# A selective-scan layer on one core: the chunks' preparation moved a batch ahead through DRAM, and one route less for the output sum

## The chip, the cores and the metric

The kernel runs on one core of one Trainium2 chip. The metric is the device time of one execution in microseconds (us). Engines are named as in the profile: PE (TensorE matmul), PEld (its weight loads), DVE (VectorE), ACT (ScalarE), POOL (GpSimd) and SP (SyncE, which issues every DMA of this kernel). Each engine works through its own queue strictly in the order in which the program was built; what one engine needs of another it waits for at that place of the queue.

## The reference

Two layers are computed for 8 images of 56 x 56 tokens and 192 channels. Layer 0 normalizes in groups, makes q with stride 1 and k, v with stride 2 (depthwise 3 x 3 convolution, affine, 1 x 1 convolution), attends with 3 heads, projects and adds. Layer 1 is a two-dimensional selective scan, cut here to what matters:

```python
xz = jnp.einsum('bhwc,oc->bhwo', x, in_proj_w)
xa, z = jnp.split(xz, 2, axis=-1)
xc = silu(depthwise_conv3x3(xa) + conv_b)              # 384 channels
# xs: four directions k: rows, columns, and both reversed
x_dbl = jnp.einsum('bkdl,kcd->bkcl', xs, x_proj_weight)
dts, Bs, Cs = jnp.split(x_dbl, [R, R + N], axis=2)     # R = 12, N = 16 states
delta = softplus(jnp.einsum('bkrl,kdr->bkdl', dts, dt_projs_weight) + dt_projs_bias)
def step(h, inp):
    u_l, d_l, B_l, C_l = inp
    h = exp(d_l[..., None] * A) * h + d_l[..., None] * B_l[:, :, None, :] * u_l[..., None]
    return (h, jnp.sum(h * C_l[:, :, None, :], axis=-1))
# y: the four directions' outputs brought back to one order, plus xs * Ds, and summed
y = layernorm(y) * out_norm_w + out_norm_b
x = x + einsum(y * silu(z), out_proj_w)
```

The scan has 3136 steps for each of 8 images, 4 directions, 384 channels and 16 states.

## The kernel before

**Tiling.** The 384 channels are three blocks of 128 partitions (NJ = 3). The 3136 tokens are seven chunks of 448 (NCH, T), a chunk is four pieces of 112 (SUB, TP). The main loop goes over 224 steps: batch, direction k, chunk. The reversed directions (k = 2, 3) go through the chunks backwards and through the columns of a chunk by negative strides. A state n of a chunk is a [128, 3 x 448] tile.

**One state.** SP loads row B_n, broadcast to 128 partitions (bb, L643, 4 buffers). POOL multiplies it with du = delta * u into dbu (L652, 3 buffers). ACT computes exp(A_n * delta) for each channel block into PSUM (da, L657, 2 banks). DVE runs the recurrence (tensor_tensor_scan, L659) from da and dbu into h (4 buffers); its last column is copied by ACT into newc (L662), the start of the next chunk. Then `add_state` forms sum over n of h * C_n in PSUM (y, one set of three banks), by one of three routes:

- BY_DVE, states 0, 6, 11: PE broadcasts row C_n to PSUM with a selection matrix (cm, L647), DVE multiplies h by it in place (L598), PE adds h to y through the identity (L604).
- BY_POOL, states 3, 8, 13: C_n is loaded broadcast (cb, L650), POOL multiplies in place (L601, once for each block), PE adds as above (L604).
- the other ten: for each of four pieces of 112 tokens PE transposes the three blocks of h into one bank (ht, L611), ACT copies that bank to SBUF scaled by C_n, which is now a per-partition scalar (g, L613), and PE transposes back and adds into y (L615).

After the last state DVE adds y into yacc, which holds the sum of directions in SBUF (L690 for direction 0, three instructions; L693 otherwise, one).

**Preparation.** `prepare` makes delta, du, B and C of one chunk of one direction while the chunk before it is scanned; it is a generator of which a piece is issued after every second state. It loads xs, projects (px, L553), copies to SBUF (xd, L555), stores the 32 rows of B and C to DRAM, transposes C (pct, L563; ct, L565), makes delta's argument (pdt, L573), and computes softplus as max(x, 0) + log(1 + exp(-|x|)) with a correction: on ACT L575 (Abs), L576 (Relu), L578 (Exp), L579 (Identity), L581 (Ln), on DVE L580, L582, L583 over [128, 3 x 448], and on POOL du (L585).

**Other work.** `front(b + 1)`, everything that comes before the scan for the next image (normalization, convolutions, attention, input projection and convolution), is a generator too. Each `yield` gives a cost; after every state the main loop issues pieces of it until the costs issued reach `total * (slot - first_slot) / (NTOK - NST - first_slot)`. So it is spread evenly over a batch's slots (a slot is one state): from the eighth chunk on (first_slot = 7 x 16) in batches after the first, from the first chunk in batch 0, and up to the last chunk but one. During direction 0, `finish(b - 1)` (layer norm, gate, output projection of the image before) is woven in, two pieces a state. All of these take PSUM from one pool of three banks. The framework derives all waits from the tiles and orders each engine's queue.

Of the kernel before, what the change touches and what calls it, by code (L numbers as in the profile page):

```python
# [18 lines left out]
L = HW * HW  # L19
# [20 lines left out]
BY_DVE = (0, 6, 11)  # L40
BY_POOL = (3, 8, 13)
EPS = 1e-5
CAP = 60.0
NTOK = NDIR * NCH * NST


@with_exitstack
def kernel(
# [56 lines left out]

    sel = fill("sel", [NR, len(BY_DVE), 128], 1.0)
    for i, n in enumerate(BY_DVE):
        nc.gpsimd.affine_select(out=sel[:, i], in_=sel[:, i], compare_op=ALU.is_equal, fill=0.0,
                                base=-(R + NST + n), pattern=[[0, 128]], channel_multiplier=1)

# [6 lines left out]
    xpw = load("xpw", [128, NDIR, NJ, NR], xp_wT.rearrange("k (j p) r -> p k j r", p=128))  # L117
# [35 lines left out]
    dchunk = ctx.enter_context(tc.tile_pool(name="dchunk", bufs=2, space=DRAM))  # L153
# [18 lines left out]
    s1 = ctx.enter_context(tc.tile_pool(name="s1", bufs=1))  # L172
    s2 = ctx.enter_context(tc.tile_pool(name="s2", bufs=2))
# [58 lines left out]
    def front(b):  # L232
# [184 lines left out]
        with tc.tile_pool(name=f"fw_{b}", bufs=1) as fw, tc.tile_pool(name=f"fi_{b}", bufs=2) as fi:  # L417
# [11 lines left out]
            made[b] = dict(x1d=x1d, xcs=xcs, rstd=rstd1, nbias=nbias)  # L429

            for j in range(NJ):
# [27 lines left out]
                for c in range(NCH):  # L459
                    xw = fi.tile([128, RPC, HW], F32, name="xw")  # L460
                    nc.gpsimd.tensor_copy(xw, xv.rearrange("p (h w) -> p w h", w=HW)[:, c * RPC:(c + 1) * RPC])
                    nc.sync.dma_start(xcs[1][:, j, c * T:(c + 1) * T], xw.rearrange("p a b -> p (a b)"))
                    yield 0.05

# [75 lines left out]
    dtws = {}  # L540

    def prepare(b, k, c, i):

        xs = s2.tile([128, NJ, T], F32, name="xs")
        nc.sync.dma_start(xs, made[b]["xcs"][k % 2][:, :, c * T:(c + 1) * T])
        if i == 0:
            dtw = s2.tile([R, DIN], F32, name="dtw")
            nc.sync.dma_start(dtw, dt_wT[:, k, :])
            dtws[k] = dtw
        yield {}  # L550
        px = bank("px")
        for j in range(NJ):
            nc.tensor.matmul(px[:NR, :T], xpw[:, k, j], xs[:, j], start=(j == 0), stop=(j == NJ - 1))  # L553
        xd = s2.tile([NR, T], F32, name="xd")
        nc.scalar.copy(xd, px[:NR, :T])  # L555
        rows = dchunk.tile([2 * NST, T], F32, name="rows")
        nc.sync.dma_start(rows, xd[R:NR, :])
        st = {"xs": xs, "xd": xd, "rows": rows}
        yield st

        pct = bank("pct")
        for s in range(SUB):
            nc.tensor.transpose(pct[:TP, s * NR:(s + 1) * NR], xd[:, s * TP:(s + 1) * TP], ident[:NR, :NR])  # L563
        ct = s2.tile([TP, SUB, NST], F32, name="ct")
        nc.scalar.copy(ct, pct[:TP, :SUB * NR].rearrange("p (s r) -> p s r", r=NR)[:, :, R + NST:NR])  # L565
        st["ct"] = ct

        dl = s2.tile([128, NJ, T], F32, name="dl")
        e = s1.tile([128, NJ, T], F32, name="e")
        ln = s1.tile([128, NJ, T], F32, name="ln")  # L570
        for j in range(NJ):
            pdt = bank("pdt")
            nc.tensor.matmul(pdt[:, :T], dtws[k][:, j * 128:(j + 1) * 128], xd[0:R, :], start=True, stop=True)  # L573
            q = k * NJ + j
            nc.scalar.activation(e[:, j], pdt[:, :T], AF.Abs, bias=dtb[:, q])  # L575
            nc.scalar.activation(dl[:, j], pdt[:, :T], AF.Relu, bias=dtb[:, q])  # L576
            yield st
        nc.scalar.activation(e, e, AF.Exp, scale=-1.0)  # L578
        nc.scalar.activation(ln, e, AF.Identity, bias=one)  # L579
# [178 lines left out]
```

## Time and profile before

| | us |
|---|---|
| median of 3 runs (21,996.19 to 22,010.04) | 21,998.8 |
| the profiled execution | 21,992.22 |
| its span, first to last instruction | 21,990.5 |
| mean granted TensorE clock | 0.92 |

| group (line) | instructions' count in the profile | busy us |
|---|---|---|
| POOL dbu L652 | 3584 | 10,845.1 |
| DVE scan L659 (with and without a start value) | 10,752 | 11,586.5 |
| ACT exp L657 | 10,752 | 6,795.8 |
| ACT g L613 | 8960 | 4,786.1 |
| POOL h*C L601 | 2016 | 2,508.1 |
| DVE h*C L598 | 672 | 1,035.9 |
| DVE L580, L582, L583 | 224 each | 432.9, 404.3, 344.7 |
| ACT L575, L576, L578, L579, L581 | 672, 672, 224, 224, 224 | 422.8, 424.1, 296.2, 316.3, 296.8 |
| POOL du L585 | 224 | 679.8 |

A row of the profile gives line, engine, operation, output and inputs by the program's names, shapes and count; then busy time and the mean of one in ns; then the idle time of the engine just before such instructions and what ended most of it. A matmul of float32 stands as two records (L604: 8064 records for 4032 instructions); one that only transposes stands as one. The ends of matmuls are modelled and records on PE and ACT overlap, so a group's mean is longer than its busy time over its count. A wait view names who waited for whom, with total, number and longest.

### The profile page before, as it was taken

The numbers are of one execution on the slowest core, as the hardware profiler recorded it, in microseconds if no ns is written. First come the engines' busy times: TensorE is split into PE (matmuls) and PEld (weight loads), VectorE is DVE, ScalarE is ACT, GpSimd is POOL, SyncE is SP. The second block draws the span as 40 slices with busy tenths as digits, with TensorE's granted clock in tenths as the row PEclk, the third lists the DMA queues.
The fourth block names the chain that finished last, engine by engine and source line by source line (L and its number), as shares of the span: only waits on it lengthen the run. The fifth ranks groups of instructions, "written<-read, shape, count | busy, mean of one in ns | idle before, by whom it ended". The sixth has DMA issues, their size and how long they took to land. (4 is left out here: it accounts for less than half of the span.)

```text
span 21990.5 us, 246125 instructions
## 1 busy us (share of the span) xinstructions
PE 18854.4 (86%) x84640; PEld 11005.3 (50%) x84640; DVE 15390.6 (70%) x14585; ACT 14548.1 (66%) x28166; POOL 14468.7 (66%) x6131
## 2 busy tenths in 40 slices
PE   8889888899888998889888899888988889887776
PEld 4454555545455455554555545555455554554444
DVE  1477777766677666876677766777667776677775
ACT  2467667666675766757666676666767667677665
POOL 0467677666676667766677666776667666677775
PEclk9899999999999999999999999999999999998888
DMA  1222222222222222222223222222222222222221
GB/s 50 82 66 66 67 84 65 74 62 65 82 68 71 63 69 77 81 61 61 73 75 80 60 62 73 76 77 62 61 84 68 76 61 61 81 70 67 61 61 41
DMA packets 935285, 1508.59 MB, mean 69 GB/s; under 512 B 102480, under 2 KB 917904, under 8 KB 930960
## 3 DMA queue, kind: packets, MB, share of 16 engines
q1 hardware_dynamic: 934032, 1492.83, 24.3%
q8 instruction: 670, 10.98, 0.2%
q14 instruction: 583, 4.78, 0.1%
HBM read 1322.38 MB, written 170.08 MB: 68 GB/s over the span
## 5 line engine op out<-in xcount | busy, mean ns | idle before, releaser
L652 POOL TENSOR_TENSOR dbu<-du,bb 128x1344 f32<-128x1344 f32 x3584 | 10845.1, 3040 | 4585.7 <-DVE h L659 2376.8
L659 DVE TENSOR_TENSOR_SCAN h<-da,newc,dbu 128x448 f32<-128x448 f32 x9216 | 10006.9, 1134 | 4142.2 <-PE ht L611 1467.0
L657 ACT ACTIVATE da<-dl,acoef 128x448 f32<-128x448 f32 x10752 | 6795.8, 638 | 3454.9 <-DVE h L659 3423.1
L613 ACT ACTIVATE g<-ht,ct 112x384 f32<-112x384 f32 x8960 | 4786.1, 576 | 1364.1 <-PE ht L611 1331.2
L615 PE MATMUL y<-ident,g 112*128 112x112 f32 x26880 | 4360.3, 281 | 1316.2 <-ACT g L613 1276.1
L611 PE MATMUL ht<-ident,h 128*112 128x128 f32 x26880 | 4483.0, 288 | 671.5 <-DVE h L659 182.1
L615 PEld LDWEIGHTS y<-ident,g 112*128 112x128 f32 x26880 | 2994.2, 147 | 3629.3 <-ACT g L613 3017.1
L604 PE MATMUL y<-h,ident 128*128 128x448 f32 x8064 | 3805.4, 611 | 473.2 <-DVE h L598 207.5
L611 PEld LDWEIGHTS ht<-ident,h 128*112 128x112 f32 x26880 | 3213.5, 141 | 1978.7 <-issue 1012.7
L601 POOL TENSOR_TENSOR h<-h,cb 128x448 f32<-128x448 f32 x2016 | 2508.1, 1272 | 1374.7 <-ACT newc L662 1374.7
L604 PEld LDWEIGHTS y<-h,ident 128*128 128x128 f32 x8064 | 1588.3, 211 | 2092.7 <-issue 1472.4
L659 DVE TENSOR_TENSOR_SCAN h<-da,dbu 128x448 f32<-128x448 f32 x1536 | 1579.6, 1072 | 676.2 <-PE ht L611 209.2
L662 ACT COPY newc<-h 128x3 f32<-128x3 f32 x3584 | 702.9, 196 | 1267.6 <-DVE h L659 1260.8
L215 PE MATMUL pcv<-xa,dg 128*128 128x440 f32 (+2 forms) x3024 | 1303.0, 545 | 0.3 <-ACT g L613 0.3
L388 PE MATMUL ps<-qT,kT 64*112 64x448 f32 x2352 | 1160.3, 605 | 70.3 <-DMA qT<-qd 38.3
L598 DVE TENSOR_TENSOR h<-h,cm 128x1344 f32<-128x1344 f32 x672 | 1035.9, 1542 | 255.8 <-PE cm L647 244.2
L396 PE MATMUL po<-pT,vt 112*128 112x448 f32 x2352 | 1043.1, 550 | 0.0
L585 POOL TENSOR_TENSOR du<-dl,xs 128x1344 f32<-128x1344 f32 x224 | 679.8, 3035 | 540.6 <-DVE dl L583 526.2
L391 ACT ACTIVATE pT<-ps,nsh 112x448 f32<-112x448 f32 x1176 | 726.1, 630 | 290.9 <-PE ps L388 237.8
L215 PE MATMUL pq<-band,dgq 96*96 96x440 f32 (+3 forms) x2016 | 866.4, 546 | 0.0
L647 PE MATMUL cm<-xd,sel 44*128 44x448 f32 x1344 | 712.0, 611 | 6.5 <-ACT dl L576 6.5
L573 PE MATMUL pdt<-xd,dtw 12*128 12x448 f32 x1344 | 708.0, 607 | 0.0
(140 smaller groups left out, 12929.0 us busy)
## 6 DMA issues: line engine op xcount, KB each, us to landing
bb<-rows SPq DMA_DIRECT2D x3584, 224.0 KB
cb<-rows SPq DMA_DIRECT2D x672, 224.0 KB
xt<-x1d SPq DMA_DIRECT2D x224, 336.0 KB
xs<-xch SPq DMA_DIRECT2D x112, 672.0 KB
xs<-xcw SPq DMA_DIRECT2D x112, 672.0 KB
xch<-xv SPq DMA_DIRECT2D x24, 1568.0 KB
xcw<-xw SPq DMA_DIRECT2D x168, 224.0 KB
xin<-in_x_dram SPq DMA_DIRECT2D x56, 336.0 KB
```

What stands on the lines that cost most here:

```text
L215: nc.tensor.matmul(out[:, o0:o1, a:b], lhs, img(lo, hi)[:, :, a + dx - 1:b + dx - 1], start=(t == TAPS[0]), stop=(t == TAPS[-1]))
L388: nc.tensor.matmul(ps[:TP, :T], kh[rows, kb * TP:(kb + 1) * TP], qh[rows, :], start=True, stop=True)
L396: nc.tensor.matmul(po[:, :T], vt[:, kb, g:g + 2, :].rearrange("p g d -> p (g d)"), pts[kb], start=(kb == 0), stop=(kb == NKB - 1))
L598: nc.vector.tensor_tensor(h, h, cm[:, :T].unsqueeze(1).to_broadcast([128, NJ, T]), ALU.mult)
L601: nc.gpsimd.tensor_tensor(h[:, j], h[:, j], cm, ALU.mult)
L604: nc.tensor.matmul(y[:, j, :T], ident, h[:, j], start=(n == 0), stop=(n == NST - 1))
L611: nc.tensor.transpose(ht[:TP, j * 128:(j + 1) * 128], h[:, j, cols], ident)
L613: nc.scalar.activation(g, ht[:TP, :DIN], AF.Copy, scale=ct[:, s, n:n + 1])
L615: nc.tensor.matmul(y[:, j, cols], g[:, j * 128:(j + 1) * 128], ident[:TP, :TP], is_transpose=True, start=False, stop=(n == NST - 1 and s = ...
L652: nc.gpsimd.tensor_tensor(dbu, du, bb.unsqueeze(1).to_broadcast([128, NJ, T]), ALU.mult)
L657: nc.scalar.activation(da[:, :T], dl[:, j], AF.Exp, scale=acoef[:, k * NJ + j, n:n + 1])
L659: nc.vector.tensor_tensor_scan(h[:, j, rev], da[:, 0:T][:, rev], dbu[:, j, rev], 0.0 if ci == 0 else carry[:, j, n:n + 1], ALU.mult, ALU.add)
```

## The change

What it does:

- `prepare` becomes `prep(b, lay, c, pools)`: one chunk in one layout (rows or columns) for both directions of that layout (k = lay and lay + 2). One projection serves both: xpw holds the two directions' weights side by side in 2 x 64 columns, so direction i's results lie on partitions 64 i and up; dtw is kept in SBUF in the same manner. The maximum max(x, 0) is computed by DVE, and so is the copy of ct. delta (dl), du, the rows of B and C, and ct are written to DRAM.
- The preps of image b + 1 (14: two layouts, seven chunks) run in the filler behind `front(b + 1)`, in the same even spread by costs; it ends a chunk earlier (NTOK - 2 * NST, and what is left is issued after the last chunk but two). Before the loop, `front(0)` and the first three preps of image 0 are issued; its other eleven come first in batch 0's filler.
- The scan loads each chunk's dl, du and ct from DRAM (`load_chunk`, at state 4 of the chunk before; xs too for direction 0).
- POOL writes du * B_n straight into an h tile, the scan runs in place, and there are ten h tiles (s8) in place of four h and three dbu.
- BY_DVE is gone, with its selection matrix and cm; BY_POOL is now states 0, 5, 10. The other thirteen take the transposing route. For BY_POOL states POOL, not ACT, copies newc.

```diff
-BY_DVE = (0, 6, 11)
-BY_POOL = (3, 8, 13)
+BY_POOL = (0, 5, 10)
 EPS = 1e-5
 CAP = 60.0
 NTOK = NDIR * NCH * NST
+HBUFS = 10
+LEAD = 3
...
+    xpw = fill("xpw", [128, 2, NJ, 2, 64], 0.0)
+    for k in range(NDIR):
+        nc.sync.dma_start(xpw[:, k % 2, :, k // 2, :NR], xp_wT[k].rearrange("(j p) r -> p j r", p=128))
+    dtw = const.tile([128, 2, DIN], F32, name="dtw")
+    for k in range(NDIR):
+        nc.sync.dma_start(dtw[k // 2 * 64:k // 2 * 64 + R, k % 2], dt_wT[:, k, :])
...
+            made[b] = dict(
+                x1d=x1d, xcs=xcs, rstd=rstd1, nbias=nbias,
+                dl=[dbatch.tile([128, NJ, L], F32, name=f"dl{k}") for k in range(NDIR)],
+                du=[dbatch.tile([128, NJ, L], F32, name=f"du{k}") for k in range(NDIR)],
+                rows=[dbatch.tile([2 * NST, L], F32, name=f"rows{k}") for k in range(NDIR)],
+                ct=[dbatch.tile([TP, L // TP, NST], F32, name=f"ct{k}") for k in range(NDIR)])
...
+    def prep(b, lay, c, pools):
+        p1, p2 = pools
+        m = made[b]
+        cols = slice(c * T, (c + 1) * T)
+        xs = p2.tile([128, NJ, T], F32, name="xs")
+        nc.sync.dma_start(xs, m["xcs"][lay][:, :, cols])
+        px = bank("px")
+        for j in range(NJ):
+            nc.tensor.matmul(px[:, :T], xpw[:, lay, j].rearrange("p k r -> p (k r)"), xs[:, j],
+                             start=(j == 0), stop=(j == NJ - 1))
+            yield 0.75
+        xd = p2.tile([128, T], F32, name="xd")
+        nc.scalar.copy(xd, px[:, :T])
+        pct = bank("pct")
+        for s in range(SUB):
+            nc.tensor.transpose(pct[:TP, s * 128:(s + 1) * 128], xd[:, s * TP:(s + 1) * TP], ident)
+        ct = p2.tile([TP, 2, SUB, NST], F32, name="ct")
+        nc.vector.tensor_copy(ct, pct[:TP, :].rearrange("p (s k r) -> p k s r", k=2, r=64)[:, :, :, R + NST:NR])
+        for i in range(2):
+            k = lay + 2 * i
+            nc.sync.dma_start(m["rows"][k][:, cols], xd[i * 64 + R:i * 64 + NR, :])
+            nc.sync.dma_start(m["ct"][k][:, c * SUB:(c + 1) * SUB], ct[:, i])
+        yield 0.5
+        dls, es = [], []
+        for i in range(2):
+            dls.append(p2.tile([128, NJ, T], F32, name="dl"))
+            es.append(p2.tile([128, NJ, T], F32, name="e"))
+        for j in range(NJ):
+            pdt = [bank("pdt") for _ in range(2)]
+            for i in range(2):
+                nc.tensor.matmul(pdt[i][:, :T], dtw[i * 64:i * 64 + R, lay, j * 128:(j + 1) * 128],
+                                 xd[i * 64:i * 64 + R, :], start=True, stop=True)
+            for i in range(2):
+                q = (lay + 2 * i) * NJ + j
+                nc.scalar.activation(es[i][:, j], pdt[i][:, :T], AF.Abs, bias=dtb[:, q])
+                nc.vector.tensor_scalar(dls[i][:, j], pdt[i][:, :T], dtb[:, q], 0.0, ALU.add, ALU.max)
+            yield 1.0
+        for i in range(2):
+            k = lay + 2 * i
+            e, dl = es[i], dls[i]
+            nc.scalar.activation(e, e, AF.Exp, scale=-1.0)
+            du = p2.tile([128, NJ, T], F32, name="du")
+            nc.scalar.activation(du, e, AF.Identity, bias=one)
+            nc.vector.scalar_tensor_tensor(e, du, -1.0, e, ALU.add, ALU.subtract)
+            yield 0.1
+            nc.scalar.activation(du, du, AF.Ln)
+            nc.vector.tensor_tensor(dl, dl, e, ALU.subtract)
+            nc.vector.tensor_tensor(dl, dl, du, ALU.add)
+            nc.sync.dma_start(m["dl"][k][:, :, cols], dl)
+            yield 0.1
+            nc.gpsimd.tensor_tensor(du, dl, xs, ALU.mult)
+            nc.sync.dma_start(m["du"][k][:, :, cols], du)
...
+    def load_chunk(b, k, c, i):
+        m = made[b]
+        cols = slice(c * T, (c + 1) * T)
+        dl = s2.tile([128, NJ, T], F32, name="dl_s")
+        nc.sync.dma_start(dl, m["dl"][k][:, :, cols])
+        du = s2.tile([128, NJ, T], F32, name="du_s")
+        nc.sync.dma_start(du, m["du"][k][:, :, cols])
+        ct = s2.tile([TP, SUB, NST], F32, name="ct_s")
+        nc.sync.dma_start(ct, m["ct"][k][:, c * SUB:(c + 1) * SUB])
+        xs = None
+        if k == 0:
+            xs = s1.tile([128, NJ, T], F32, name="xs_s")
+            nc.sync.dma_start(xs, m["xcs"][0][:, :, cols])
+        return dl, du, ct, xs
...
     def add_state(n, h, cm, y, ct):
 
-        if n in BY_DVE:
-            nc.vector.tensor_tensor(h, h, cm[:, :T].unsqueeze(1).to_broadcast([128, NJ, T]), ALU.mult)
-        elif n in BY_POOL:
+        if n in BY_POOL:
             for j in range(NJ):
                 nc.gpsimd.tensor_tensor(h[:, j], h[:, j], cm, ALU.mult)
...
+    def preps(b, todo):
+        es, pools = prep_pools(b)
+        with es:
+            for lay, c in todo:
+                yield from prep(b, lay, c, pools)
+    chunks = [(lay, c) for lay in range(2) for c in range(NCH)]
+    main = sum(front(0))
+    each = sum(preps(0, chunks[:LEAD])) / LEAD
...
+            late = preps(0, chunks[LEAD:]) if b == 0 else iter(())
+            fill = itertools.chain(front(b + 1), preps(b + 1, chunks)) if b + 1 < nb else iter(())
+            if b == 0:
+                fill = itertools.chain(late, fill)
+            total = main + len(chunks) * each + (each * (len(chunks) - LEAD) if b == 0 else 0.0)
...
-                dbu = s3.tile([128, NJ, T], F32, name="dbu")
+                    nc.sync.dma_start(cm, rows[NST + n, cols].partition_broadcast(128))
+                h = s8.tile([128, NJ, T], F32, name="h")
                 nc.gpsimd.tensor_tensor(
-                    dbu, du, bb.unsqueeze(1).to_broadcast([128, NJ, T]), ALU.mult)
-                h = s4.tile([128, NJ, T], F32, name="h")
+                    h, du, bb.unsqueeze(1).to_broadcast([128, NJ, T]), ALU.mult)
                 for j in range(NJ):
                     da = pa.tile([128, 512], F32, name="da")
                     nc.scalar.activation(da[:, :T], dl[:, j], AF.Exp,
                                          scale=acoef[:, k * NJ + j, n:n + 1])
                     nc.vector.tensor_tensor_scan(
-                        h[:, j, rev], da[:, 0:T][:, rev], dbu[:, j, rev],
+                        h[:, j, rev], da[:, 0:T][:, rev], h[:, j, rev],
                         0.0 if ci == 0 else carry[:, j, n:n + 1], ALU.mult, ALU.add)
-                nc.scalar.copy(newc[:, :, n:n + 1], h[:, :, last])
+                (nc.gpsimd.tensor_copy if n in BY_POOL else nc.scalar.copy)(newc[:, :, n:n + 1], h[:, :, last])
...
+            if n == 4 and i + 1 < len(steps):
+                nxt = load_chunk(*steps[i + 1])
...
-                want = total * (slot - first_slot) / (NTOK - NST - first_slot)
+                want = total * (slot - first_slot) / (NTOK - 2 * NST - first_slot)
...
-        if k == NDIR - 1 and ci == NCH - 2:
+        if k == NDIR - 1 and ci == NCH - 3:
```

## The prediction

> **What bounds the kernel now.** I read the page's totals first, then the busy time of the engines in the stages of one batch, then the rows of the costliest groups, and last the waits of a stage without foreign work.
>
> ```profile
> span 21990.5 us, 246125 instructions
> PE 18854.4 (86%) x84640; PEld 11005.3 (50%) x84640; DVE 15390.6 (70%) x14585; ACT 14548.1 (66%) x28166; POOL 14468.7 (66%) x6131
> ```
>
> No engine is full over the whole run, so the average does not say what an edit is worth. The stages do. A batch is 28 chunks of 16 states; the closing yacc instructions (L690, L693) mark where each ends. The next view sums busy time over stretches between such ends; columns are the stretch, its length, then PE, PEld, DVE, ACT and POOL busy, clock, DMA share, GB/s. The first three are batch 4: seven chunks of direction 0 with the previous batch's finish, the chunk in which the next batch's front starts, and 19 chunks with front work. The last is 20 chunks of batch 7: scan and preparation alone.
>
> ```profile
> 11381.70:11976.00 594.30, 500.55 (x2486) 313.77 (x2486) 474.96 (x457) 445.15 (x854) 469.33 (x196) 0.95 0.27 71
> 11976.00:12110.40 134.40, 97.50 (x482) 65.14 (x482) 98.44 (x116) 66.94 (x131) 73.84 (x32) 0.84 0.35 94
> 12110.40:13979.90 1869.50, 1671.62 (x7329) 944.39 (x7329) 1286.54 (x1194) 1253.16 (x2428) 1207.17 (x511) 0.94 0.24 67
> ...
> 20038.10:21730.10 1692.00, 1266.13 (x5960) 752.10 (x5960) 1298.11 (x1102) 1153.90 (x2300) 1227.09 (x522) 0.84 0.22 61
> ```
>
> Per chunk: 84.9 us in the first stage (PE fullest, 71.5), 98.4 in the third (PE 88.0, gap 10.4), 84.6 in the last (DVE 64.9, POOL 61.4, PE 63.3, ACT 57.7, so a gap of 20). Front chunks are near a PE bound; the others are held by waits between engines. In the last stage these are (us in total, times, longest):
>
> ```profile
> POOL dbu L652 <- DVE h L659: 230.0, 97, 4.2
> PEld ht L611 <- issue: 219.7, 257, 4.6
> DVE h L659 <- ACT da L657: 218.6, 167, 5.8
> PEld y L604 <- POOL h L601: 184.3, 180, 2.7
> ```
>
> PE waits in its queue for GpSimd's h*C (L601, behind multiplies that wait for one of three dbu tiles); the transposes behind it are late, then ACT's scaled copies, then the exponentials behind those, and the scan waits for ACT: some 11 us a chunk.
>
> **Scan, part by part.** Prices are busy time over count from these rows (records overlap a little, so I apply them to differences of measured busy time only):
>
> ```profile
> L613 ACT ACTIVATE g<-ht,ct 112x384 f32<-112x384 f32 x8960 | 4786.1, 576 | 1364.1 <-PE ht L611 1331.2
> L615 PE MATMUL y<-ident,g 112*128 112x112 f32 x26880 | 4360.3, 281 | 1316.2 <-ACT g L613 1276.1
> L611 PE MATMUL ht<-ident,h 128*112 128x128 f32 x26880 | 4483.0, 288 | 671.5 <-DVE h L659 182.1
> ...
> L604 PE MATMUL y<-h,ident 128*128 128x448 f32 x8064 | 3805.4, 611 | 473.2 <-DVE h L598 207.5
> ...
> L598 DVE TENSOR_TENSOR h<-h,cm 128x1344 f32<-128x1344 f32 x672 | 1035.9, 1542 | 255.8 <-PE cm L647 244.2
> ```
>
> Three states a chunk move from VectorE to the transposing route. PE gains 36 transpose pairs at 0.329 us, 11.8, and loses 18 matmul passes at 0.472, 8.5, and the cm broadcast, 3.2: nothing on balance. ACT gains 12 copies at 0.534, 6.4, and gives three newc copies (0.196 each) to GpSimd. DVE loses 4.6. The preparation leaves the chunk: 6.2 on PE, 8.6 on ACT, 7.4 on DVE (in the last stage), 3.0 on GpSimd. A 3-element copy on GpSimd is in no row: 0.1 us by its 1-element memsets, 0.48 by its 448-element ones; nearer to the first, 0.3. The scan in place keeps its shape, 1.08 us: nothing, hidden or not; at worst it is slower by what is unpriced here. What is left of a bare chunk: POOL 59.3, PE 57.2, ACT 54.9, DVE 52.9. The floor is 59.3 and the ceiling today's 84.6. Ten h tiles replace four h and three dbu, so the multiplies ahead of h*C no longer wait for a scan just done, but GpSimd still does h*C in turn, and PE and ACT still stand behind it three times a chunk: I take a gap of 12.7, so **72**. Direction 0: PE 71.5 - 6.1 = 65.4, POOL 64.9; gap 13 as today (84.9 - 71.5): **78.5**.
>
> **Where the preparation goes.** A prep (one chunk, two directions) now counts 6.35 units in the filler; the front counts 572. Together 661 units are spread over 19 chunks (7 to 25), where 572 had 20. So the front gets 16.4 chunks and all 14 preps are squeezed into 2.6, about chunks 24 to 26; the built order of the changed program shows them just there. But the units are PE time. A prep costs DVE 2 x (1.93 + 1.80 + 1.54) for L580, L582, L583 (their means over the run), 6 x 0.67 for the maximum that leaves ACT (nearest row: L442, same shape from PSUM; the other end is ACT's own 0.63) and 0.2 for ct: 14.8; ACT 12.4; PE 9; GpSimd 6.1. Three such chunks hold 3 x 52.9 + 14 x 14.8 = 366 us of DVE work and 338 of ACT work, 122 a chunk, where a chunk takes 98 today. 366 is the floor. The ceiling is the stage whose DVE is fullest today, the 134.4 us chunk, at 1.37 us per busy us: 500. Direction 0 has 1.19, bare chunks 1.30; I take 1.25: **457**. What is late next: PE idles there for lack of work, its front work having been done earlier, at a higher density.
>
> **Front chunks.** PE 88.0 - 6.1, and the front 20/16.4 denser: its share is 25 (88.0 - 63.3) to 35 (the rows of its lines, 5683 us over 8 x 20 chunks), so +5.4 to +7.6; I take 88.4. The gap is between 3 (y has one set of banks, and the built order puts yacc behind the first scan of state 9 of the next chunk, so the next y waits for a multiply, 3.0, that scan, 1.1, and yacc, 2.3, some 3 us more than PE has to do meanwhile) and today's 10.4. Ten tiles let the scan lead by nine states, which feeds PE; each ACT copy still stands in line with exponentials. I take 7.6: **96**. The chunk where the front starts loses 9.9 us of DVE: 125.
>
> A later batch: 7 x 78.5 + 125 + 16 x 96 + 457 + 72 = 2740, against 2683 as the mean of batches 1 to 6: +57, six times +342. Batch 7: 549.5 + 21 x 72 = 2061.5, against 2377.9: -316.
>
> **Batch 0** does 25 preps. Before its first scan stand two of them and a trip through DRAM, where one direction took 22.3 us:
>
> ```profile
> 738.83 0.53 ACT L555 COPY xd<-px 44x448 f32<-44x448 f32 x1 [13.68 <-PE px L553]
> ...
> 749.39 1.55 DVE L580 SCALAR_TENSOR_TENSOR e<-ln,e 128x1344 f32<-128x1344 f32 x1
> ...
> 761.16 2.07 DVE L659 TENSOR_TENSOR_SCAN h<-da,dbu 128x448 f32<-128x448 f32 x2 [3.58 <-POOL dbu L652]
> ```
>
> +10 (two DMA trips of 5.0, as xs took from its issue at 729.10 to PE's start on it at 734.11) to +60 (both preps in series): 36, first scan at 797. Eleven preps in the first three chunks: 1.25 x (3 x 52.9 + 163) = 402. Twenty front chunks at 88 (PE 88.4 less 7, as the front spreads over 20.3 chunks there, and a gap of 7) and 27 more for the one where it starts (125 against 98): 1787. Fourteen preps in four chunks: 1.25 x 419 = 524. One bare chunk. 3582, against 3328.9: +253.
>
> **DMA, SP, constants.** Writing and reading dl and du adds 617 MB and the shared xs saves 39: q1 goes from 24.3% to about 34%, no bound. SP issues about 217 instead of 60 of these per batch, all in order: in a prep chunk its stores, waiting for DVE and GpSimd, stand between the bb loads. Four bb tiles cover 12 us; that is part of the 1.25. The constants' eight small loads for two lie under the first front's 740 us of other work: nothing, or some 5 us (one DMA trip) without that cover.
>
> [...] L580 takes 1.55 alone, 1.93 on average, and in bare chunks
>
> ```profile
> L580 DVE SCALAR_TENSOR_TENSOR e<-ln,e 128x1344 f32<-128x1344 f32 x20 | 87.7, 4385 | 3.9 <-ACT ln L579 3.9
> ```
>
> which is one GpSimd multiply (3.04) more. [...]
>
> **Sum.** +342 + 253 - 316 = +279 on the span of 21,990.5: 22,269.5, and 1.7 outside it as in the profiled run (21,992.2 in all), 22,271. The median, 21,998.8, is 6.6 above that run; I leave it out.
>
> **Rivals.** *Ten tiles close the gaps* (faster): one mechanism, the lead of the scan. Gap 4.6 in front chunks (93), 10 in direction 0 (75), 9 in bare ones (68), preps at 1.05: a batch 2583, batch 0 3368, batch 7 1953; 21,007. For it: waits, not work, fill the gaps. Against: GpSimd's h*C stays in all queues. It decides once front chunks (116 of them) average under 93.5, other terms as forecast. *The chain of a prep binds* (slower still): dl, e and du have two buffers, both used by one prep, so the next waits for its stores: 16.0 us from xd to dl (738.83 to 754.9), 3.0 du, 5.0 store, 6 for the second direction is 30 on idle engines, 40 in queues; 14 x 40 = 560 for 457, and 25 x 7.4 in batch 0: 23,073. Against: the region overlaps preps' ends. *The tiles stay unused*: GpSimd's newc copy and h*C wait for the scan in its own queue, chunks stay 84.6 and 84.9: +28 x 12.6 + 49 x 6.4, 22,938. Against: in bare chunks the built order puts ten multiplies ahead of the first copy.
>
> **How the numbers follow.** Forecast 0.37, long chain 0.13, unused tiles 0.09: slower 0.59. Closed gaps 0.33. Within 0.2% (44 us, about what this measurement can tell) 0.08: forecast and rival in balance. Range 21,300 to 23,000; the forecast's own, preps at 1.15 to 1.4 of 2937 us, is 21,980 to 22,710.
>
> **What would show it.** Chunks 24 to 26 of a middle batch at 140 to 165 us with DVE over 115 busy; front chunks at 94 to 98, bare ones 68 to 76, direction 0 76 to 81; batch 7 near 2060. Prep chunks under 130 us or front chunks under 93 make it wrong.

## The result: slower by 16%, and the profile after

The changed kernel takes 25,476 us (median of 4 runs, 25,455 to 25,496) against 22,000.5 for the kernel before (4 runs): a ratio of 1.158, 95% interval 1.156 to 1.160. The direction is the one that had most of the chance; the time lies far outside the range.

The page's totals of the changed kernel:

```profile
span 25453.5 us, 275939 instructions
...
PE 19586.6 (77%) x94272; PEld 12662.8 (50%) x94272; DVE 15296.1 (60%) x14697; ACT 15379.5 (60%) x29174; POOL 14650.3 (58%) x6800
```

DVE and POOL have about as much to do as before, ACT 6% more, and all three are less full: what grew there is waiting. The stages of batch 4, cut within 3 us of the ends of the yacc instructions (columns: stretch, length, then PE, PEld, DVE, ACT and POOL busy, clock, DMA share, GB/s): seven chunks of direction 0, the chunk where the next front starts, 15 front chunks, three chunks that hold the preps; the last line is 21 bare chunks of batch 7, with neither front work nor preps.

```profile
13708.80:14280.40 571.60, 454.63 (x2718) 337.85 (x2718) 416.10 (x413) 428.60 (x840) 446.25 (x210) 0.90 0.33 88
14280.40:14423.40 143.00, 99.11 (x540) 70.19 (x538) 102.01 (x129) 76.44 (x156) 69.46 (x39) 0.84 0.32 91
14423.40:16230.00 1806.60, 1439.66 (x6541) 902.28 (x6542) 888.02 (x885) 988.87 (x1933) 897.05 (x434) 0.87 0.22 63
16230.00:16770.00 540.00, 381.32 (x1338) 218.14 (x1337) 413.34 (x322) 333.81 (x521) 303.35 (x118) 0.65 0.39 130
23833.00:25266.00 1433.00, 1032.25 (x6933) 742.22 (x6933) 1118.34 (x1030) 1164.13 (x2372) 1207.38 (x579) 0.95 0.30 81
```

Per chunk, by the ends themselves, forecast in brackets: direction 0 81.8 (78.5); first front chunk 143 (125); front chunks 120.3 (96); the three prep chunks 540 (457); bare chunks 68.2 (72). Batches 1 to 6 take 3189 on average (2740), batch 0 4125 (3582), batch 7 2007 (2061.5). So the bare chunks went even better than foretold, and of the 452 us by which batch 4 was missed 328 stand in its front chunks and the bare ones at its end together (15 of 120.3 and two of 65.6, where 16 of 96 and one of 72 were foretold), 83 in the preps, 41 in the first eight chunks. A front chunk holds 96.0 us of PE and a gap of 24.3; 88.4 and 7.6 were foretold.

The two rows of product and scan show what is late:

```profile
L687 POOL TENSOR_TENSOR h<-du_s,bb 128x1344 f32<-128x1344 f32 x3584 | 11025.8, 3087 | 8189.4 <-PE ht L638 3294.4
L693 DVE TENSOR_TENSOR_SCAN h<-da,newc,h 128x448 f32<-128x448 f32 x9216 | 10063.5, 1135 | 7307.8 <-POOL h L687 5595.9
```

Product and scan last about as long as before (3.09 us for 3.04, 1.14 for 1.14); the idle time in front of them is new. GpSimd's product waits for PE, the scan for the product.

### The profile page after: what moved, and what is told of

The parts are those of the page before. It is cut to its first block, busy times and chain, and to the rows that moved or that the text cites. A ratio compares the mean times of both kernels' runs of the same rounds, so it can differ in the third digit from the quotient of the medians.

```text
span 25453.5 us, 275939 instructions
## 1 busy us (share of the span) xinstructions
PE 19586.6 (77%) x94272; PEld 12662.8 (50%) x94272; DVE 15296.1 (60%) x14697; ACT 15379.5 (60%) x29174; POOL 14650.3 (58%) x6800
## 5 line engine op out<-in xcount | busy, mean ns | idle before, releaser
L687 POOL TENSOR_TENSOR h<-du_s,bb 128x1344 f32<-128x1344 f32 x3584 | 11025.8, 3087 | 8189.4 <-PE ht L638 3294.4
L693 DVE TENSOR_TENSOR_SCAN h<-da,newc,h 128x448 f32<-128x448 f32 x9216 | 10063.5, 1135 | 7307.8 <-POOL h L687 5595.9
L691 ACT ACTIVATE da<-dl_s,acoef 128x448 f32<-128x448 f32 x10752 | 6796.2, 637 | 5512.6 <-DVE h L693 5474.5
L642 PE MATMUL y<-ident,g 112*128 112x112 f32 x34944 | 6119.0, 297 | 2989.5 <-ACT g L640 2927.0
L640 ACT ACTIVATE g<-ht,ct_s 112x384 f32<-112x384 f32 x11648 | 6192.4, 574 | 1686.8 <-PE ht L638 1499.7
L642 PEld LDWEIGHTS y<-ident,g 112*128 112x128 f32 x34944 | 4262.5, 158 | 5787.6 <-ACT g L640 4984.6
L638 PE MATMUL ht<-ident,h 128*112 128x128 f32 x34944 | 6287.1, 304 | 1021.0 <-ACT pT L393 217.6
L638 PEld LDWEIGHTS ht<-ident,h 128*112 128x112 f32 x34944 | 4535.6, 149 | 2273.4 <-issue 900.5
L631 PE MATMUL y<-h,ident 128*128 128x448 f32 x4032 | 2014.5, 634 | 541.3 <-DVE yacc L725 290.2
L693 DVE TENSOR_TENSOR_SCAN h<-da,h 128x448 f32<-128x448 f32 x1536 | 1573.6, 1072 | 1203.2 <-POOL h L687 915.9
```

What stands on the lines that cost most here:

```text
L631: nc.tensor.matmul(y[:, j, :T], ident, h[:, j], start=(n == 0), stop=(n == NST - 1))
L638: nc.tensor.transpose(ht[:TP, j * 128:(j + 1) * 128], h[:, j, cols], ident)
L640: nc.scalar.activation(g, ht[:TP, :DIN], AF.Copy, scale=ct[:, s, n:n + 1])
L642: nc.tensor.matmul(y[:, j, cols], g[:, j * 128:(j + 1) * 128], ident[:TP, :TP], is_transpose=True, start=False, stop=(n == NST - 1 and s = ...
L687: nc.gpsimd.tensor_tensor(h, du, bb.unsqueeze(1).to_broadcast([128, NJ, T]), ALU.mult)
L691: nc.scalar.activation(da[:, :T], dl[:, j], AF.Exp, scale=acoef[:, k * NJ + j, n:n + 1])
```

## Experiments

### Where the front chunks' time went: a closed ring

Each single run below had the kernel before beside it, at 21,980 to 22,057 us, so differences of some 0.3% between single runs tell nothing.

The waits in 15 front chunks, first of the kernel after, then in the 19 of the kernel before (who waited for whom; total us, times, longest):

```profile
DVE h L693 <- POOL h L687: 841.3, 212, 8.6
ACT da L691 <- DVE h L693: 576.0, 354, 6.3
PEld y L642 <- ACT g L640: 371.0, 392, 5.9
POOL h L687 <- PE ht L638: 315.8, 71, 11.4
```

```profile
ACT da L657 <- DVE h L659: 344.7, 394, 6.6
PEld y L615 <- ACT g L613: 270.4, 414, 4.3
POOL dbu L652 <- DVE h L659: 262.1, 108, 9.6
DVE h L659 <- PE ht L611: 235.0, 106, 8.9
```

Before, GpSimd's product waited mostly for the scan, and the scan for PE. Now the product waits for PE, and the scan for the product. The timeline of the kernel after in two such states (start, length, instruction, in brackets the idle time before it and who ended it):

```profile
15203.13 3.23 DVE L693 TENSOR_TENSOR_SCAN h<-da,newc,h 128x448 f32<-128x448 f32 x3 [4.51 <-POOL h L687]
...
15207.74 0.42 PE L638 MATMUL ht<-ident,h 128*112 128x128 f32 x1
...
15208.30 3.03 POOL L687 TENSOR_TENSOR h<-du_s,bb 128x1344 f32<-128x1344 f32 x1 [5.20 <-ACT da L691]
...
15211.36 3.23 DVE L693 TENSOR_TENSOR_SCAN h<-da,newc,h 128x448 f32<-128x448 f32 x3 [5.00 <-POOL h L687]
15212.55 0.64 ACT L691 ACTIVATE da<-dl_s,acoef 128x448 f32<-128x448 f32 x1 [1.39 <-DVE h L693]
...
15213.96 2.42 PE L631 MATMUL y<-h,ident 128*128 128x448 f32 x6
...
15216.46 3.04 POOL L687 TENSOR_TENSOR h<-du_s,bb 128x1344 f32<-128x1344 f32 x1 [5.14 <-PE y L631]
...
15219.53 3.23 DVE L693 TENSOR_TENSOR_SCAN h<-da,newc,h 128x448 f32<-128x448 f32 x3 [4.94 <-POOL h L687]
```

PE ends a state's last transpose at 15208.16; 0.14 us later the product starts (the view names an exponential of ACT there, which no product reads), and 0.03 us after the product's end at 15211.33 the scan. The next product starts 0.08 us after PE's six passes over an h tile. Product and scan take turns, 8.2 us a state, each engine idle for 5.

My theory: a tile that the product and the scan share is freed by PE's read. In front chunks PE runs behind, and the built order lets the scan's queue run nine states ahead of PE's, the whole ring of ten tiles (they are used in turn, so a state writes over the tile of the state ten earlier). Then product (s + 10) waits for PE's read of state s, scan (s + 10) for the product, the exponentials behind it for the scan, and ACT's scaled copies g, which stand in ACT's queue behind those exponentials, hold PE. (In the trace of the changed kernel the instructions that name a tile, 14,697 on DVE, 29,013 on ACT and 6796 on GpSimd, all stand in the built order.) In bare chunks PE follows one or two states behind, and the ring should hold nothing up.

The trace of the changed kernel shows the wait itself. By the order of their records, 85% of the products of these 15 chunks start within 0.5 us of PE's last read of the state ten earlier (median 0.14 us, none sooner than 0.08). In bare chunks 45% do so too, but there the scan leads PE by 2.0 states on average, for 9.6 in front chunks, and the products run some eight ahead of the scan, so it doesn't wait for them.

Four runs tell the theory from its rivals. The first takes back the sharing in the changed kernel:

```diff
-HBUFS = 10
+HBUFS = 7
-                h = s8.tile([128, NJ, T], F32, name="h")
+                dbu = s3.tile([128, NJ, T], F32, name="dbu")
                 nc.gpsimd.tensor_tensor(
-                    h, du, bb.unsqueeze(1).to_broadcast([128, NJ, T]), ALU.mult)
+                    dbu, du, bb.unsqueeze(1).to_broadcast([128, NJ, T]), ALU.mult)
+                h = s8.tile([128, NJ, T], F32, name="h")
...
-                        h[:, j, rev], da[:, 0:T][:, rev], h[:, j, rev],
+                        h[:, j, rev], da[:, 0:T][:, rev], dbu[:, j, rev],
```

> The changed kernel with the scan out of place again: GpSimd's product goes to one of three dbu tiles, the scan writes one of seven h tiles (ten tiles in all, as in the changed kernel). Theory (closed ring): in the changed kernel the product for state s+10 may not start before PE has read state s, so product (3.1 us), scan (1.1 to 3.4), exponential and scaled copies stand in series with PE, about 7.5 us a state. Out of place, the product waits only for the scan three states earlier: front chunks fall from 120 to 95..102 us, the whole from 25,476 to 23,000..23,700. Rival (three more states on the transposing route load ACT's queue and PE): front chunks stay at 115 or more, the whole within 1.5% of 25,476. Bare chunks tell how much of their 68 us is owed to the place: with the ring open there, 68..70 by the theory.

Measured, one run: 22,597 us. The stages of batch 4, 15 front chunks and three prep chunks, and 21 bare chunks of batch 7:

```profile
12646.70:14088.60 1441.90, 1274.33 (x6544) 797.17 (x6544) 887.24 (x884) 984.89 (x1932) 897.27 (x434) 0.96 0.28 79
14088.60:14578.50 489.90, 368.29 (x1340) 215.15 (x1340) 380.52 (x322) 334.10 (x522) 293.00 (x112) 0.68 0.44 142
20800.60:22409.00 1608.40, 1126.15 (x6930) 798.10 (x6930) 1116.96 (x1028) 1165.57 (x2370) 1222.02 (x585) 0.87 0.27 73
```

Two of its waits in front chunks (12,649 to 14,166 us):

```profile
DVE h L694 <- PE ht L638: 387.0, 153, 28.6
POOL dbu L687 <- DVE h L694: 301.2, 117, 18.4
```

The product waits for the scan again, and the scan for PE. Front chunks take 96.1 us, as the theory had it; the whole lies below its 23,000, since the preps (490 for 540), direction 0 (79.3) and batch 0 (3686) gained too. The bare chunks speak against it in one point: 76.6, not 68 to 70. That is taken up below. The second run shortens the lead without opening the ring:

```diff
-HBUFS = 10
+HBUFS = 5
```

> The changed kernel with five h tiles for ten. Theory (closed ring): the built order uses up whatever tiles there are (the scan's queue leads the transposes by four states instead of nine), so the product still stands behind PE's read of the state five earlier, and front chunks stay at 112..130 us, the whole at 25,000..26,500. Rival (a lead of nine states is too long, ACT's scaled copies stand behind too many exponentials): with a lead of four, front chunks come near the 98.4 of the kernel before, the whole to 23,000..23,700.

Measured, one run: 25,574 us. The same two stages, 15 front chunks and 21 bare ones:

```profile
14469.60:16285.30 1815.70, 1442.83 (x6540) 900.02 (x6540) 883.93 (x884) 986.34 (x1930) 897.48 (x434) 0.87 0.22 63
23945.70:25382.80 1437.10, 1037.73 (x6930) 744.05 (x6930) 1116.97 (x1027) 1163.13 (x2370) 1221.44 (x584) 0.95 0.31 82
```

121.0 and 68.4 us a chunk: half the tiles make no difference of note anywhere. Between five and ten, it is neither the length of the lead nor the number of tiles; with five, 86% of the products of front chunks start within 0.5 us of PE's read of the state five earlier. The next two change one part each in the kernel before: product and scan share its seven tiles; and no h*C on VectorE, with GpSimd's three states moved to 0, 5 and 10.

```diff
+    s8 = ctx.enter_context(tc.tile_pool(name="s8", bufs=7))
...
-                dbu = s3.tile([128, NJ, T], F32, name="dbu")
+                h = s8.tile([128, NJ, T], F32, name="h")
                 nc.gpsimd.tensor_tensor(
-                    dbu, du, bb.unsqueeze(1).to_broadcast([128, NJ, T]), ALU.mult)
-                h = s4.tile([128, NJ, T], F32, name="h")
+                    h, du, bb.unsqueeze(1).to_broadcast([128, NJ, T]), ALU.mult)
...
-                        h[:, j, rev], da[:, 0:T][:, rev], dbu[:, j, rev],
+                        h[:, j, rev], da[:, 0:T][:, rev], h[:, j, rev],
```

> The kernel before with another part of the change alone: the product and the scan share one of seven h tiles (as many as four h and three dbu). Theory (closed ring): front chunks rise from 98.4 to 112..122 us, the whole to 23,500..24,600, and the wait of the scan for GpSimd's product appears as the largest one. Rival (place does not matter; preparation or the transposing route does): within 2% of 22,000.

```diff
-BY_DVE = (0, 6, 11)
-BY_POOL = (3, 8, 13)
+BY_DVE = ()
+BY_POOL = (0, 5, 10)
```

> The kernel before with one part of the change alone: no h*C on VectorE (those three states go the transposing route), GpSimd's three states are 0, 5 and 10. Theory (closed ring by the scan in place): here the product still goes to dbu, freed by the scan, so front chunks stay at 95..103 us for 98.4 and the whole within 2% of 22,000 (21,700..22,400). Rival (the longer transposing route is what costs): front chunks at 115..120, the whole at 24,000..24,700.

Measured, one run each: 24,120 and 21,450 us, beside 21,986 for the kernel before. Sharing alone costs 2134 us. Its stretch of 15 front chunks, and two of its waits there:

```profile
13376.10:15114.00 1737.90, 1480.35 (x5834) 824.06 (x5834) 1010.38 (x964) 1010.63 (x1950) 921.37 (x393) 0.85 0.20 54
```

```profile
DVE h L659 <- POOL h L653: 640.6, 149, 10.1
...
POOL h L653 <- PE ht L612: 314.0, 79, 11.5
```

115.9 us a chunk, with the two waits of the changed kernel, though preparation, routes and number of tiles are those of the kernel before. The longer transposing route is no loss but a gain of 2.4%: 18 front chunks of batch 4 take 95.3 us for 98.6, bare ones 81.0 for 84.1, direction 0 88.7 for 84.9. Repeated, to have an interval:

> The kernel before without h*C on VectorE again, to have an interval: 21,450 +-0.3%, a ratio of 0.975 +-0.003 to the kernel before.

21,432 us (median of 4 runs), ratio 0.974, interval 0.973 to 0.976. Taken apart in this order, the parts come to about -0.54 thousand (the route), +1.15 (preparation ahead, its room and GpSimd's newc: 22,597 less 21,450) and +2.88 (sharing: 25,476 less 22,597; alone in the kernel before it was 2.13).

### Why bare chunks got 68 us: the order in GpSimd's queue

```diff
-HBUFS = 7
+HBUFS = 5
-                dbu = s3.tile([128, NJ, T], F32, name="dbu")
+                dbu = s3.tile([128, NJ, T], F32, name="dbu", bufs=5)
```

> The changed kernel out of place, with five dbu and five h tiles for three and seven. Theory (the lead of the products): bare chunks took 68 us in place and 77 out of place because GpSimd's products could run ten states ahead and here only three; with five, bare chunks fall to 69..73, batch 7 from 2169 to 2010..2090, while front chunks stay at 93..98 since the product still waits for a scan, not for PE; the whole 22,250..22,480. Rival (it is the scan's lead of nine states that fills the bare chunks): bare chunks stay at 76 or more, or rise, as the scan's lead falls to four.

Measured, one run: 22,578 us, bare chunks 76.2, front chunks 96.3. The products' lead is not it, against the theory, and neither is the scan's: with five tiles for ten the changed kernel had 68.4. The timeline of GpSimd with three dbu and seven h tiles, in a bare chunk:

```profile
21518.29 0.19 POOL L697 COPY newc<-h 128x3 f32<-128x3 f32 x1 [0.99 <-DVE h L694]
21518.44 3.03 POOL L687 TENSOR_TENSOR dbu<-du_s,bb 128x1344 f32<-128x1344 f32 x1
21521.42 3.32 POOL L629 TENSOR_TENSOR h<-h,cb 128x448 f32<-128x448 f32 x3
```

Between newc and h*C of one state the built order puts a product: the scan that ends frees a dbu tile too, and h*C, which overwrites h, also waits for the copy. So h*C comes 3.0 us late, three times a chunk. In the changed kernel a scan's end frees no tile for a product, and in its bare chunks h*C follows at once:

```profile
24518.62 0.19 POOL L696 COPY newc<-h 128x3 f32<-128x3 f32 x1 [0.67 <-DVE h L693]
24518.89 3.31 POOL L629 TENSOR_TENSOR h<-h,cb 128x448 f32<-128x448 f32 x3
```

This holds throughout the 21 bare chunks: a product stands between the two in all 63 cases out of place, with three dbu tiles as with five, and in none of the changed kernel, with ten tiles or five. From the end of a state's last scan to h*C it is 3.2 us out of place and 0.3 in the changed kernel. I gave h*C a tile of its own, so that it waits for the scan alone (against the run before):

```diff
-                dbu = s3.tile([128, NJ, T], F32, name="dbu", bufs=5)
+                dbu = s3.tile([128, NJ, T], F32, name="dbu", bufs=4)
...
+            hc = s1.tile([128, NJ, T], F32, name="hc")
             for j in range(NJ):
-                nc.gpsimd.tensor_tensor(h[:, j], h[:, j], cm, ALU.mult)
+                nc.gpsimd.tensor_tensor(hc[:, j], h[:, j], cm, ALU.mult)
...
-                (nc.gpsimd.tensor_copy if n in BY_POOL else nc.scalar.copy)(newc[:, :, n:n + 1], h[:, :, last])
+                nc.scalar.copy(newc[:, :, n:n + 1], h[:, :, last])
```

Five h, four dbu and one hc make the ten tiles.

> The changed kernel out of place, four dbu and five h tiles, and h*C on GpSimd writes a tile hc of its own instead of h; all newc copies on ACT. Theory (order in GpSimd's queue): out of place, the built order puts one more product (3.0 us) between the newc copy and h*C of the same state, because the dbu tile and h*C become free by the same scan and h*C also waits for the copy; that is 3 x 3.0 = 9 us a chunk, the 77 - 68 that bare chunks lost against the changed kernel. With hc the built order has h*C first. Then bare chunks fall to 67..72, batch 7 from 2160 to 1980..2080, the whole from 22,578 to 22,000..22,450. Rival (it is the writing in place itself, or the number of products ahead): bare chunks stay at 75 or more and the whole within 0.4% of 22,578.

Measured, one run: 22,900 us, beyond the theory's 22,450. GpSimd's timeline in a bare chunk, and 15 front and 21 bare chunks:

```profile
22001.44 3.35 POOL L630 TENSOR_TENSOR hc<-h,cb 128x448 f32<-128x448 f32 x3
22004.74 9.07 POOL L688 TENSOR_TENSOR dbu<-du_s,bb 128x1344 f32<-128x1344 f32 x3
```

```profile
12930.60:14474.00 1543.40, 1315.42 (x6544) 839.18 (x6544) 885.19 (x884) 990.29 (x1977) 891.27 (x389) 0.91 0.26 74
21280.40:22709.10 1428.70, 1057.95 (x6930) 763.16 (x6930) 1118.28 (x1028) 1174.58 (x2432) 1207.43 (x519) 0.95 0.30 82
```

Bare chunks fall to 68.0 out of place: writing in place is not what they had gained by, an early h*C is. The edit does more than change the order, though: h*C now starts 2.3 us before the state's last scan ends, each block behind its own scan, newc is back on ACT, and PE reads hc, not h; these were not separated. But front chunks rise from 96.3 to 102.9, more than it is worth. The same in the kernel before, without its h*C on VectorE (against that run; the room comes from one score tile and one xd), and then for the last batch alone (against the first of the two):

```diff
+            hc = s1.tile([128, NJ, T], F32, name="hc")
             for j in range(NJ):
-                nc.gpsimd.tensor_tensor(h[:, j], h[:, j], cm, ALU.mult)
+                nc.gpsimd.tensor_tensor(hc[:, j], h[:, j], cm, ALU.mult)
```

> The kernel before without h*C on VectorE (GpSimd's three states 0, 5, 10), and h*C on GpSimd into a tile hc of its own; for the room the attention keeps seven score tiles for eight and xd one buffer for two. Theory (order in GpSimd's queue, as for the run beside it): h*C comes 3.0 us earlier three times a chunk: bare chunks of batch 7 fall from 81 to 72..77, the whole from 21,450 to 20,950..21,330. Rival (PE and ACT set these chunks, the seven score tiles or xd bring a new wait): 21,380 or more.

```diff
-            hc = s1.tile([128, NJ, T], F32, name="hc")
+            hc = s1.tile([128, NJ, T], F32, name="hc") if own else h
...
-                add_state(*done[n - 1], y, ct)
+                add_state(*done[n - 1], y, ct, b == nb - 1 and k > 0)
```

> As the kernel with hc for h*C (no h*C on VectorE, seven score tiles, one xd), but hc is used only in directions 1 to 3 of the last batch; elsewhere GpSimd's h*C overwrites h. It tells what raised front chunks from 95.5 to 100 us there. Theory (an early h*C delays the next product, which front chunks, with PE behind, don't need): front chunks come back to 95..97, a middle batch to 2620..2645, batch 7 stays at 2205..2235, the whole 21,300..21,420. Rival (the seven score tiles or the one xd): front chunks stay at 99 or more, the whole 21,750 or more.

The first: 21,945 us, above even the rival's 21,380; bare chunks 76.4 for 81.0, as the theory had it, but 18 front chunks of batch 4 100.5 for 95.3. The second, with the same room but hc in the last batch's directions 1 to 3 alone: middle batches back to 2625 (2712 with hc everywhere), batch 7 2227, and 21,342 us (median of 5 runs), ratio 0.971, interval 0.969 to 0.973. So hc itself costs time in front chunks, not the room it was given. That it delays the next product there is my reading and was not isolated. This is the lowest time of all; the mixture below, one run at 0.970 of the kernel before beside it, isn't told apart from it.

### The preps

> The changed kernel out of place, with each prep counted at 2.3 times its units in the filler: the 14 preps of a batch are spread over about 5.3 chunks instead of 3, and the front's work is squeezed into about 13.7 chunks instead of 16.4. Theory (the time goes where the work is, and squeezing it costs little by itself): front chunks rise to 102..109, prep chunks fall to 110..125, a middle batch stays at 2758 +-50, the whole at 22,250..22,950. Rival (the squeeze itself costs, preps wait for each other's two buffers and for PE): a middle batch falls under 2690, the whole under 22,150.

```diff
-                yield from prep(b, lay, c, pools)
+                for got in prep(b, lay, c, pools):
+                    yield got * PREP_WEIGHT
```

Measured, one run: 23,205 us. 12 front chunks average 103.9, the six chunks with preps behind them 121.9, both inside the theory's numbers; a middle batch is not, it rose by 85, from 2759 to 2844, and the whole lies above 22,950. Spreading the preps by this much costs more than squeezing them; that the squeezed front is the reason is my reading.

> The changed kernel with the scan out of place (three dbu, seven h tiles), and each prep's load of xs issued one prep earlier. Theory (a queue on SP): the load of xs stands behind loads of bb that wait for products, so PE's first matmul of a prep waited 43 us once in chunk 0 and 26 us once in the prep chunks of a middle batch, with all of PE's queue behind it. Then the first three chunks of batch 0 (1298 us together with the start) lose 30..45 us, the three prep chunks of a batch fall from 487 to 450..475, the whole from 22,597 to 22,300..22,490. Rival (the engines are busy or wait for each other there anyway): within 0.3% of 22,597.

`ahead` issues the load of xs for the prep that follows:

```diff
     def prep(b, lay, c, pools, xs, ahead):
-        xs = p2.tile([128, NJ, T], F32, name="xs")
-        nc.sync.dma_start(xs, m["xcs"][lay][:, :, cols])
...
+        ahead()
         xd = p2.tile([128, T], F32, name="xd")
```

Measured, one run: 22,582 us, for 22,597; the runs can't tell these two apart. PE's wait for xs in the prep chunks stayed as well (23.6 us once, 24.1 without the edit): it belongs to the first prep of a batch, whose load the edit doesn't move before the front's end. By the end of batch 0's third chunk the run was 4.5 us ahead. The theory's saving did not come; what that one wait costs was not tried.

### A mixture

> The kernel before with what the runs so far were worth, each where it paid: no h*C on VectorE except in the chunks of direction 0 that carry the previous batch's finish (89 us without it, 85 with it), and in the last batch's directions 1 to 3 product and scan share one tile, taken in turn from the seven there are. Theory: 21,450 - 49 x 4 - 21 x 8 = 21,090, range 20,950..21,300, with the bare chunks of batch 7 at 71..75. Rival (in place closes the ring in bare chunks too when there are only seven tiles and the preparation stands in the chunk): bare chunks at 81 or more, the whole at 21,250 or more.

```diff
+        by_dve, by_pool = (BY_DVE, BY_POOL) if k == 0 and b > 0 else ((), POOL_ONLY)
...
+                if place:
+                    turn = (i * NST + n) % 7
+                    dbu = s3.tile([128, NJ, T], F32, name="dbu") if turn in (1, 3, 5) else \
+                        s4.tile([128, NJ, T], F32, name="h")
```

Measured, one run: 21,387 us, above the theory's range. Direction 0 gave part of what was expected (middle batches 2612 for 2629, 17 us of 28). Shared tiles in the last batch gave nothing: its bare chunks take 83 us for 81. The rival is right there; why seven shared tiles gained in the kernel before (78.1 for 84.1) and lose here stays open. The trace names a place, not a cause: h*C of state 0 starts 7.6 us after its scan there, those of states 5 and 10 0.36 us (medians).

## Why the prediction was wrong

**The step that failed** is one sentence under "Scan, part by part": "The scan in place keeps its shape, 1.08 us: nothing, hidden or not; at worst it is slower by what is unpriced here." The duration was right. What I didn't ask is who frees the tile. Out of place GpSimd's product waited for a scan; in place it waits for PE. That is a new wait, with every later product and h*C queued behind it on GpSimd, the scan behind these, and ACT's scaled copies behind the exponentials that wait for the scan. It was put at nothing and cost 25,476 - 22,597, some 2.9 of the 3.2 thousand us that the forecast missed. The same assumption came back under "Front chunks": "Ten tiles let the scan lead by nine states, which feeds PE". The lead of nine states is the ring used up: the scan leads by nine because PE is nine behind. The gap of 7.6 was bounded by today's 10.4, a gap of a kernel whose products wait for scans; it was 24.3. With the ring opened, the changed kernel has 96.1 a front chunk (96 foretold), 85.0 on PE and 11.2 of gap: that the sum fits so well is luck, since PE came out 3.4 under the 88.4 foretold and the gap 3.6 over its 7.6, beyond even its bound of 10.4.

**The other terms**, with the ring open (three dbu, seven h) and in the changed kernel:

| term | foretold | ring open | changed kernel |
|---|---|---|---|
| front chunk | 96 | 96.1 | 120.3 |
| direction 0, a chunk | 78.5 | 79.3 | 81.8 |
| chunk where the front starts | 125 | 129 | 143 |
| three prep chunks | 457 | 490 | 540 |
| bare chunk | 72 | 76.6 | 68.2 |
| middle batch | 2740 | 2759 | 3189 |
| batch 0 | 3582 | 3686 | 4125 |
| batch 7 | 2061.5 | 2169 | 2007 |
| whole span | 22,269.5 | 22,595.5 | 25,453.5 |

- *Preps.* Work and factor were nearly right: 380.5 us of DVE for 366, and 490/380.5 = 1.29 for 1.25. One reading behind the 1.25 was wrong: direction 0's 1.19 is us per busy us of PE, over DVE it is 594.3/474.96 = 1.25. In the changed kernel the ring stands in the prep chunks too.
- *VectorE beside GpSimd's multiplies.* L526 and L527 rose from the 1.80 and 1.54 I had priced:

```profile
L526 DVE TENSOR_TENSOR dl<-dl,e 128x1344 f32<-128x1344 f32 x224 | 667.8, 2989 | 4.5
L527 DVE TENSOR_TENSOR dl<-dl,du 128x1344 f32<-128x1344 f32 x224 | 618.3, 2767 | 23.2 <-ACT du L525 15.2 <-ACT xd L491 0.5 <-DVE dl L526 0.5
```

  By their own records, 139 of the 224 L526 start while a GpSimd multiply runs (a product, or du of a prep); they last 3.87 us on average, and 135 of them end 1.42 us after that multiply. The other 85 last 1.55. In the kernel before 74 of 224 started so (L582). L523, at 1.75, stayed below its 1.93: 124 of the 150 that overlap a multiply started before it and lasted 1.55, and the multiply took 4.0 us instead of 3.0. The three together take 7.5 us a direction, 4.66 at 1.55 each. No run here moves the multiplies away from them, so why they last longer is not shown.
- *Bare chunks.* The number was near, the reason wrong: not the tiles, but h*C in front of the next product.
- *Batch 0.* The first scan began at 795.4 (797 foretold). The first three chunks then took 536 us (402). PE stood for a prep's xs for 43 us there, a load that SP issued at 851.1, behind stores of dl and du and loads of bb; I had seen that order on SP and put it into the factor 1.25. What it costs by itself is open.
- *Rivals.* "Ten tiles close the gaps" needed front chunks under 93.5. "The tiles stay unused" kept bare chunks at 84.6; they fell. "The chain of a prep binds" had 560 for the preps, near the 540, but with the ring open they took 490, and spreading them out gained nothing; no run here points to the two buffers, though their number was not varied.
- *The direction* came out as foretold, but mostly for another reason. The sum of the forecast's own parts was +279; with the ring open they came to about +0.6 thousand.

## What to carry to other kernels

When an operation is put in place, ask for each tile who frees it before and after: if a producer used to wait for its neighbour and now waits for the last reader, it joins that reader's ring, and more buffers don't open the ring where the queues' order uses them all. Price such an edit in the stage where the reader lags, not where it keeps up: the same edit took 8 us from a bare chunk and added 24 to a front chunk. And read the order in which an engine issues two instructions that come free together; one product of 3 us in front of h*C, three times a chunk, was worth all that sharing seemed to bring.

## What the hardware showed that I had not expected

PE's granted clock differed by stage, and not with how busy PE was. The same front work kept PE busy for 85.0 us a chunk at a clock of 0.96 with the ring open, and for 96.0 at 0.87 with it closed. So 11 of the 24 us that a front chunk grew by stand as busy time of PE; the ratio of the two clocks would give about 9 of them (85.0 x 0.96/0.87 = 93.8, an estimate). Yet in the changed kernel PE is busy for 71% of the prep chunks at 0.65, and for 72% of the bare chunks at 0.95.

What goes with the clock in these six stages is how much of the time lies in long gaps. By PE's records, gaps of over 2 us make up 4.5% of the front chunks at 0.96, 7% of the bare chunks at 0.95, 12% of the front and 13% of the bare chunks at 0.87, and 15% and 22% of the prep chunks at 0.68 and 0.65. No run here isolates the clock from the waits.
